# A message-passing layer on one core: an earlier first round of grouped edges, later list and node preparation, three accumulators for four, and four buffers for small sums

## The chip, the cores and the metric

The kernel runs on one core of a Trainium2 chip. The metric is the device time of one execution in microseconds (us). Three runs of the kernel before gave 2089.85, 2090.91 and 2092.94 us, a median of 2090.91. One more execution was recorded by the profiler; all traces below are of such recorded executions.

## What is computed

```python
h = relu(layernorm(x))                      # x: 6250 nodes x 128 features, f32
hw = h @ W_in
W_ij = (softplus(f_ij @ W_f1 + b_f1) - log 2) @ W_f2 + b_f2
W_ij = W_ij * cutoff                        # f_ij: 200000 edges x 20
out = segment_sum(hw[dst] * W_ij, src)      # per edge: gather by dst, sum by src
x + (softplus(out @ W_o1 + b_o1) - log 2) @ W_o2 + b_o2
```

The names follow the kernel's inputs. The list of edges is sorted by `dst`, so the gather of `hw` reads a narrow, moving window of rows. `src` is random, so the sum by `src` goes to rows all over the table of nodes.

## The kernel before

**Units of work.** 128 edges are a chunk, four chunks are a quad (512 edges); there are 391 quads, and one iteration of the main loop starts one quad. Two quads share a load of features, a load of window offsets and four loads of node rows (`load_sc`, L287 to L308), which SP issues two iterations or more ahead.

**A quad's way.** `s1_pe` (L313) multiplies the features with W_f1 in the iteration before; ACT takes exponential and logarithm (L318, L323); `s2_pe_x` and `s2_pe_w` (L494 to L505) gather the node rows by a one-hot matrix and multiply with W_f2; ACT scales by the cutoff (L510); DVE multiplies both (`s2_m`, L520). The message m, 512 edges x 128, is then summed by `src` in one of three ways:

- *Plain quads* (`plainq`): edges with equal `src` within a chunk are summed on PE by an equality matrix (`s3_pe`, L532), copied by ACT (L540), and scattered with addition into an accumulator in HBM: four indirect DMAs issued by POOL (`scatter`, L582).
- *Listed quads*: m goes straight to four such scatters. Edges that repeat a `src` within their column have been given a place in a side list of 128 rows per 16 quads, prepared ahead (`l_eq`, `l_count`, `l_index`, `l_place`) and summed and scattered later (`l_sum`, `l_copy`, with one `os` buffer).
- *Grouped quads*: no scatter of the quad. `src` is cut into 16 groups of 392 nodes. Ranks within a group are prepared for eight quads at once (`rank_group` to `rank_slot`). DVE builds a permutation (`perm_oh`, L662) and splits m into three bf16 parts (`part_rem`, L676), PE permutes the edges so that 32 slots belong to each group (`permute`, L687), and ACT copies (L693). Edges over 32 of a group go to 64 overflow slots (`over_pe`, L702 to L704), are summed in pairs of quads (`over_row`, `over_sum`) and leave as one scatter, through an `os` buffer (`over_copy`, L746). After eight grouped quads, a *round*, four *units* run (`unit_pe`, L781): each adds four groups of all eight quads on PE, and DVE adds the result into `accT` in SBUF (`unit_evac`, L792; L790 in the first round).

So a grouped quad costs matmuls and about half a scatter, and the other kinds cost four scatters and few matmuls.

**Which quad is what.** `sorted_quads` fixes the grouped ones: from 8 on with gaps 2, 2, 2, 3, so 8, 10, 12, 14, 17 and so on to 383, 168 in all; quads 0 to 7 and 384 to 390 are not grouped. `unit_slots` gives the iterations of the units: 28, 32, 37, 41 in the first round, 389, 391, 393, 395 in the last. Of the 223 other quads the middle 192 are listed and 31 are plain (12 at the beginning, 19 at the end).

**What sets the order.** The order on each engine is written out by hand: in iteration i the fixed steps run, and between them hooks at named points (`at(i, point, fn)`; `"L"` for loads, `"D0"` to `"D2"` on DVE, `"PE2"` for the grouped work on PE, `"A0"` to `"A2"` on ACT, `"S"` for scatters). Every engine works strictly in this order. SP issues nearly all loads and stores, POOL the scatters.

**Accumulators.** `NACC = 4` tables of all nodes lie in HBM and take the scatters in turn, so that one scatter does not wait for the landing of the one before (`acc_of`: the first 2 go to table 0, up to 8 to tables 0 and 1, up to 140 to tables 0 to 2, then to all four; the last 64 go to tables 1 to 3, while table 0 is added into `accT` during the loop: `r0_load` to `r0_add`). All are zeroed at the start from a zeroed piece of `accT`: tables 0 and 1 from POOL in the prologue, 2 and 3 by ten SP transfers of 128x640 f32 each (`zero_piece`), the side lists by three each (`zero_list`).

**Preparation of node rows.** `prep_stat` to `prep_x3` normalise 256 nodes, multiply with W_in and write three bf16 parts to a table; the steps of group g start at iteration `prep_start(g)`: 6, 15, 24 and so on for groups 1, 2, 3.

**The end.** After the loop two flags are loaded by every engine (L1272, L1278), which choose fallback code that this input does not need. Then an output stage over 13 groups of 512 nodes loads tables 1 to 3 (`t_load`, L1356), adds them (`t_sum1`, `t_sum2`, L1362, L1368), transposes, adds `accT`, and does the last two layers (L1373 to L1419).

## Time and profile before

| | us |
|---|---|
| runs: lowest, median, highest | 2089.85, 2090.91, 2092.94 |
| the profiled execution's own time | 2069.4 |
| its span, first instruction to last | 2067.6 |
| PE busy | 1854.7 (90%) |
| VectorE (DVE) busy | 1657.1 (80%) |
| POOL busy | 1631.5 (79%) |
| ScalarE (ACT) busy | 1490.1 (72%) |

The span is one execution on the chip, and times in the rows are in us from its start. "busy" is the time in which an engine has an instruction; PE is TensorE's matmuls, PEld its weight loads. In a row of the timeline stand start, length, engine, line, operation, output<-inputs by the program's names, count, and in brackets the idle time before it and what ended it. In a row of waits stand who waited for whom, us in total, how often, and the longest. A group's row gives count, busy us, mean ns of one, and the idle time before.

### The profile page before, as it was taken

How to read it: one execution, taken by the hardware profiler on the slowest of the kernel's cores; microseconds unless marked ns; L12 is line 12 of the kernel's file. 1: busy time of each engine (PE TensorE's matmuls, PEld its weight loads, DVE VectorE, ACT ScalarE, POOL GpSimd, SP SyncE). 2: the span in 40 equal slices, each digit the busy share in tenths (PEclk: the TensorE clock that was granted, in tenths of full speed). 3: DMA queues.
4: the chain of work that ended last, by engine and by line, in shares of the span. 5: the costliest groups of instructions: out<-in, count | busy, mean ns of one | idle time of the engine just before them, and what ended most of it. 6: DMA issues, size and time to landing. Idle time of an engine off the chain costs nothing. (4 is left out here: it accounts for less than half of the span.)

```text
span 2067.6 us, 57535 instructions
## 1 busy us (share of the span) xinstructions
PE 1854.7 (90%) x20381; PEld 1285.7 (62%) x20381; DVE 1657.1 (80%) x4448; ACT 1490.1 (72%) x4083; POOL 1631.5 (79%) x1040
## 2 busy tenths in 40 slices
PE   3489997999999999999999999999999999999956
PEld 2356664666666666666666666666666666677734
DVE  3578896898987888988988978979889787787735
ACT  3368775777776788777778777777778678888714
POOL 3578888888877788887878878888888888888774
PEclk9689998999999999999999999999999999999978
DMA  7887766767766776766667666676676676667648
GB/s 240 227 211 150 125 124 109 128 112 135 130 124 106 126 133 117 136 124 122 121 133 123 122 123 117 118 129 107 129 128 116 112 126 111 110 120 131 129 46 242
DMA packets 381187, 272.56 MB, mean 132 GB/s; under 512 B 97727, under 2 KB 341354, under 8 KB 380898
## 3 DMA queue, kind: packets, MB, share of 16 engines
q0 software_dynamic: 143728, 71.30, 34.9%
q1 hardware_dynamic: 236882, 197.50, 33.8%
q8 instruction: 161, 2.64, 0.5%
q14 instruction: 128, 1.05, 0.2%
q10 hardware_dynamic: 288, 0.07, 0.0%
HBM read 154.45 MB, written 114.24 MB: 130 GB/s over the span
## 5 line engine op out<-in xcount | busy, mean ns | idle before, releaser
L582 POOL DMA_INDIRECT acc<-s,lji x768 | 1237.3, 1611 | 266.9 <-issue 184.6
L687 PE MATMUL pq<-pt,pm 128*128 128x387 bf16 x2688 | 527.9, 339 | 27.0 <-DVE pt L676 10.7
L510 ACT ACTIVATE xc<-xg,cb 128x128 f32<-128x128 f32 x1564 | 446.4, 371 | 121.0 <-PE xg L497 113.8
L505 PE MATMUL W<-w,a 128*128 128x128 f32 x3128 | 464.1, 293 | 0.0
L505 PEld LDWEIGHTS W<-w,a 128*128 128x128 f32 x3128 | 388.7, 196 | 42.0 <-issue 2.6
L781 PE MATMUL un<-so,mst 32*128 32x392 bf16 x8064 | 378.3, 331 | 31.9 <-ACT os L746 19.3
L693 ACT CAST mst<-pq 128x387 bf16<-128x387 f32 x672 | 303.1, 481 | 132.6 <-PE pq L687 130.0
L687 PEld LDWEIGHTS <-pm 128*128 128x128 bf16 x2688 | 259.4, 99 | 211.4 <-issue 16.7
L781 PEld LDWEIGHTS <-mst 32*128 32x128 bf16 x8064 | 228.4, 94 | 175.0 <-issue 70.0
L323 ACT ACTIVATE a<-a,con 128x512 f32<-128x512 f32 x391 | 282.3, 722 | 12.7
L582 POOL DMA_INDIRECT acc<-s,ji x123 | 197.0, 1602 | 82.8 <-issue 25.9
L318 ACT ACTIVATE a<-z 128x512 f32<-128x512 f32 x391 | 237.4, 607 | 33.2 <-PE z L313 17.4
L676 DVE TENSOR_TENSOR pt<-pt 128x512 f32<-128x512 f32 x336 | 231.8, 690 | 5.8
L662 DVE TENSOR_SCALAR pm<-iot,pos 128x576 bf16<-128x576 f16 x672 | 221.4, 390 | 0.0
L520 DVE TENSOR_TENSOR s<-W,xc 128x512 f32<-128x512 f32 x192 | 131.9, 687 | 92.9 <-ACT xc L510 86.0
L792 DVE TENSOR_TENSOR accT<-un,accT 128x392 f32<-128x392 f32 x320 | 158.5, 558 | 58.4 <-PE un L781 58.2
L766 DVE TENSOR_SCALAR so<-iot,mst 128x392 bf16<-128x392 f16 x672 | 191.2, 344 | 5.5 <-PE un L781 5.4
L582 POOL DMA_INDIRECT acc<-os,oji x96 | 155.6, 1621 | 31.1 <-issue 16.2
L497 PE MATMUL xg<-wn,oh 63*128 63x128 bf16 x1564 | 157.2, 222 | 14.5 <-ACT xc L510 8.1
L313 PE MATMUL z<-ft,ws 123*128 123x512 bf16 x391 | 151.6, 388 | 16.1 <-POOL b2rep L927 9.3
L494 PE MATMUL W<-b2rep,onesb 64*128 64x512 bf16 x391 | 153.8, 393 | 0.0
L520 DVE TENSOR_TENSOR pt<-W,xc 128x512 f32<-128x512 f32 x168 | 115.2, 686 | 34.9 <-ACT xc L510 29.4
(209 smaller groups left out, 2431.1 us busy)
## 6 DMA issues: line engine op xcount, KB each, us to landing
rb<-reld SPq DMA_DIRECT2D x391, 64.0 KB
fsd<-f SPq DMA_DIRECT2D x49, 480.0 KB
ft<-fsd SPq DMA_DIRECT2D x195, 120.0 KB
sb<-src SPq DMA_DIRECT2D x169, 128.0 KB
fb<-in_fB_dram SPq DMA_DIRECT2D x49, 320.0 KB
ft<-fsd SPq DMA_DIRECT2D x195, 80.0 KB
wn<-tab SPq DMA_DIRECT2D x782, 15.8 KB
acc<-s,lji POOLq DMA_INDIRECT x768
```

Of the source, the lines that this page charges most:

```text
L318: nc.scalar.activation(a, st[q]["z"], AF.Exp)
L323: nc.scalar.activation(a, a, AF.Ln, bias=half, scale=0.5)
L505: nc.tensor.matmul(W[:, c, :], st[q]["a"][:, c * P:(c + 1) * P], w2, start=False, stop=(c == 3))
L510: nc.scalar.mul(xc[:, c, :], st[q]["xg"][:, c, :], late["c", q // CQ][:, 4 * (q % CQ) + c:4 * (q % CQ) + c + 1])
L520: nc.vector.tensor_tensor(m[:, :, :P], st[q]["W"], st[q]["xc"], op=ALU.mult)
L582: nc.gpsimd.indirect_dma_start(out=accs[k][:rows, :], out_offset=bass.IndirectOffsetOnAxis(ap=ji, axis=0), in_=s, in_offset=None, compute_ ...
L662: nc.vector.tensor_scalar(pm[:, c], iot[:, :SLOTS], rk[r]["pos"][:, 4 * j + c:4 * j + c + 1], None, op0=ALU.is_equal)
L676: nc.vector.tensor_tensor(pt[:, :, k * P:(k + 1) * P], a, high(a), op=ALU.subtract)
L687: nc.tensor.matmul(t[:, :PW], mp[q]["pm"][:, c, s * P:(s + 1) * P], high(mp[q]["pt"][:, c:c + 1, :PW])[:, 0], start=(c == 0), stop=(c == 3))
L693: nc.scalar.copy(mp[q]["ms", s][:, :PW], mp[q].pop(("q", s))[:, :PW])
L766: nc.vector.tensor_scalar(so, iotw[:, :GN], w[:, 3 * P // 2:3 * P // 2 + 1], None, op0=ALU.is_equal)
L781: nc.tensor.matmul(ts[g][:, :GN], mp[q]["ms", s][v, k * P:(k + 1) * P], mp[q]["oh"][v], start=(q == qs[0] and k == 0), stop=(q == qs[-1] a ...
```

## The change

- `HEAD`: quads 2, 3, 5, 6, 8, 9, 11 and 12 are grouped and form the first round. The pattern with gaps 2, 2, 2, 3 begins at 15. There are 176 grouped quads (22 rounds, 88 units) and 215 others: 176 listed, 39 plain (20 at the beginning, 19 at the end). Units of the first round run in iterations 17, 21, 26 and 30; the last grouped quads are 381, 384, 386, 388 and 390, the last units run in 396, 398, 400 and 402. The head quads are permuted within one iteration (`q in HEAD`).
- The ranks of the first round are prepared from iteration 0 on.
- Lists are prepared at their ordinary distance in the first window too, from iteration 12 on (first: 6); node groups start at iteration 22 (first: 6).
- `NACC = 3`. The first 4 scatters go to table 0, up to 24 to tables 0 and 1, then to three; the last 64 go to tables 1 and 2. Table 2 is zeroed one piece per iteration in iterations 3 to 12, lists in 9 to 17.
- `t_sum1` is gone, `t_sum2` is always on POOL, and the output stage loads two tables.
- `os` has four buffers, not two.
- A small load at the start (`half_load`) uses unused columns of `accT` in place of a `pm` buffer.

```diff
+HEAD = (2, 3, 5, 6, 8, 9, 11, 12)
-MP0 = 8
+MP0 = 15
+PREP0 = 23
-NACC = 4
+NACC = 3
...
-    K1_END, K2_END, K3_END = 2, 8, 140
-    Z2, Z3 = [0,0,1,1,2,2,3,3,4,4], [5+2*j for j in range(10)]
+    K1_END, K2_END = 4, 24
+    Z2 = [3+j for j in range(10)]
...
-        w = LR // ZL
-        nc.sync.dma_start(v[:, j * w:(j + 1) * w], zero[:, :w])
+        a, b = j * LR // ZL, (j + 1) * LR // ZL
+        nc.sync.dma_start(v[:, a:b], zero[:, :b - a])
...
-        s = sp_.tile([P, 132], F32, tag="os", name="os", bufs=2)
+        s = sp_.tile([P, 132], F32, tag="os", name="os", bufs=4)
...
-        if k < K3_END:
+        if k < RET:
             return k % 3
-        if k < RET:
-            return k % 4
-        return 1 + k % 3
+        return 1 + k % 2
...
-            t_ = wk.tile([HALF, 2, SEG], I32, tag="pm", name="half")
+            o = NP - 2 * (2 - k) * SEG
+            t_ = accT[:HALF, o:o + 2 * SEG].bitcast(I32).rearrange("p (a e) -> p a e", a=2)
...
-        for j in range(ZR):
-            at(Z3[j] if spread else 0, "L", zero_piece, nc.sync, 3, j)
...
             i = mpq[RKQ * r]
+            i = max(i, 5)
             at(i - 5, "D2", rank_group, r)
...
-                i = splain[n] + 2 if w else 6 + 2 * g
+                i = splain[n] + 2
...
-                    at((0, 3, 6, 9)[k] + j + 1, "L", zero_list, k, j)
+                    at(3 * k + j + 9, "L", zero_list, k, j)
...
-            if q + 4 in units:
+            if q + 4 in units or q in HEAD:
...
-        def t_sum1(g):
-            T = tgroups[g][1]
-            a2 = tl[g][2]
-            nc.gpsimd.tensor_tensor(a2[:, :T], a2[:, :T], tl[g][3][:, :T], op=ALU.add)
...
-            eng = nc.vector if g % 2 else nc.gpsimd
-            eng.tensor_tensor(a1[:, :T], a1[:, :T], tl[g][2][:, :T], op=ALU.add)
+            nc.gpsimd.tensor_tensor(a1[:, :T], a1[:, :T], tl[g][2][:, :T], op=ALU.add)
...
-            for k in (1, 2, 3):
+            for k in (1, 2):
                 t_load(g, k)
...
-    qs, q = [], MP0
+    qs, q, n = [k for k in HEAD if k < nq - MPEND], MP0, 0
     while q < nq - MPEND:
         qs.append(q)
-        q += MPGAPS[(len(qs) - 1) % len(MPGAPS)]
+        q += MPGAPS[n % len(MPGAPS)]
+        n += 1
...
-    busy = unit_its(sorted_quads(4 * PREP_GAP * (g + 8)))
-    return clear(7 + PREP_GAP * (g - 1), busy, 2) - 1
+    busy = unit_its(sorted_quads(4 * PREP_GAP * (g + 10)))
+    return clear(PREP0 + PREP_GAP * (g - 1), busy, 2) - 1
```

More of the change, by code (lines that the diff above doesn't have):

```diff
@@ L744, in over_copy @@
     def over_copy(q):
-        s = sp_.tile([P, 132], F32, tag="os", name="os", bufs=2)
+        s = sp_.tile([P, 132], F32, tag="os", name="os", bufs=4)
         nc.scalar.copy(s[:, :P + 4], mp[q].pop("sum")[:, :P + 4])
@@ L1429, in tile_gnn @@
             if TAIL_AHEAD <= j + TAIL_AHEAD < TG:
-                for k in (1, 2, 3):
+                for k in (1, 2):
                     t_load(j + TAIL_AHEAD, k)
             if j + 1 < TG:
-                t_sum1(j + 1)
                 t_sum2(j + 1)
```

## The prediction

> **What bounds the kernel now.** I read the span first, then a table of busy time by stretch, cut where the pace changes.
>
> ```profile
> span 2067.6 us, 57535 instructions
> ```
>
> ```profile
> 24.40:156.50 132.10, 83.37 (x571) 61.37 (x572) 78.14 (x202) 69.71 (x194) 76.55 (x59) 0.78 0.86 233
> 156.50:344.90 188.40, 176.04 (x1914) 121.04 (x1914) 161.47 (x443) 147.94 (x411) 154.42 (x97) 0.99 0.73 134
> 344.90:377.10 32.20, 17.83 (x197) 11.65 (x194) 14.83 (x48) 13.43 (x40) 25.68 (x18) 0.73 0.51 77
> 377.10:1957.50 1580.40, 1509.93 (x17062) 1044.12 (x17061) 1337.98 (x3600) 1220.77 (x3366) 1299.73 (x806) 0.99 0.69 123
> 1957.50:2013.30 55.80, 32.37 (x469) 22.98 (x467) 23.56 (x68) 8.91 (x31) 42.13 (x28) 0.83 0.42 45
> 2013.30:2067.70 54.40, 33.18 (x173) 23.21 (x173) 27.59 (x45) 25.22 (x39) 24.28 (x20) 0.81 0.87 237
> ```
>
> The columns are the stretch, its length, busy us (and instructions) of PE, PEld, DVE, ACT and POOL, the granted clock, the DMA share and GB/s. From 377.1 on PE is busy 1509.93 of 1580.40 us, 96%. Before that it is not: 63% in the first row, 55% in the third.
>
> The same stretches with only the z matmul of L313, one per iteration (quad), turn lengths into a pace:
>
> ```profile
> 24.40:156.50 132.10, 9.55 (x20) 2.31 (x21) 0.78 0.86 233
> 156.50:344.90 188.40, 15.51 (x40) 4.00 (x40) 0.99 0.73 134
> 344.90:377.10 32.20, 1.14 (x3) 0.30 (x3) 0.73 0.51 77
> 377.10:1957.50 1580.40, 125.02 (x327) 32.80 (x328) 0.99 0.69 123
> ```
>
> An iteration takes 132.1/20 = 6.6 us, then 4.7, then 10.7 (three of them), then 4.83 for the 327 that remain. So PE bounds the long part, and what can be won lies in the first 20 iterations, in the three at 345, and in the two end rows.
>
> The scatters alone (L582, POOL's only large work) show what holds the early part:
>
> ```profile
> 24.40:156.50 132.10, 67.96 (x42) 0.78 0.86 233
> 156.50:344.90 188.40, 154.42 (x97) 0.99 0.73 134
> 377.10:1957.50 1580.40, 1299.73 (x806) 0.99 0.69 123
> ```
>
> 97 scatters in 188.4 us are 1.94 us each and 806 in 1580.4 are 1.96, and POOL has about 0.35 us between two of them in both rows. POOL is nearly full everywhere; what differs is who is late. In the long part the waits show POOL waiting for its data, so PE and DVE lead:
>
> ```profile
> POOL acc L582 <- DVE s L520: 24.7, 19, 3.0
> ```
>
> At 347 it is the other way round, and PE stands still because a small sums buffer has not been scattered yet:
>
> ```profile
> 361.25 0.27 ACT L746 COPY os<-osum 128x132 f32<-128x132 f32 x1 [13.77 <-DMA acc<-os,oji]
> 361.56 6.58 PE L781 MATMUL un<-so,mst 32*128 32x392 bf16 x93 [14.18 <-ACT os L746]
> ...
> ACT os L746 <- DMA acc<-os,oji: 18.2, 2, 13.8
> ```
>
> Both os buffers wait on a POOL that carries the backlog of the first twelve, all scattered, quads. A second such wait, 18.2 - 13.8 = 4.4 us, lies later.
>
> At the end POOL decides again:
>
> ```profile
> 1954.26 1.54 POOL L582 DMA_INDIRECT acc<-s,ji  x1 [2.43 <-ACT ji L563]
> ...
> 1957.59 0.38 PE L313 MATMUL z<-ft,ws 123*128 123x512 bf16 x1
> ...
> 1996.41 1.98 DVE L792 TENSOR_TENSOR accT<-un,accT 128x392 f32<-128x392 f32 x4 [5.27 <-PE un L781]
> ...
> 2006.32 1.54 POOL L582 DMA_INDIRECT acc<-os,oji  x1 [0.30 <-issue]
> 2013.35 25.72 SPq L1356 DMA_DIRECT2D ta_in<-acc  x30
> ```
>
> The last seven quads (384 to 390) are all scattered. From 1954.26 to 2006.32 29 scatters follow each other at 52.1/28 = 1.86 us, while PE and DVE are done at 1998. The first load of the output stage comes 7.0 us after the last scatter started.
>
> **The change part by part.** Prices first, each from the groups of equal shape or, for the twelve overflow matmuls of a quad, from the first and last of them:
>
> ```profile
> L687 PE MATMUL pq<-pt,pm 128*128 128x387 bf16 x2688 | 527.9, 339 | 27.0 <-DVE pt L676 10.7 <-DVE rt L651 6.3 <-ACT mst L693 3.6
> L781 PE MATMUL un<-so,mst 32*128 32x392 bf16 x8064 | 378.3, 331 | 31.9 <-ACT os L746 19.3 <-DVE pr L627 6.8 <-ACT s L540 2.4
> L532 PE MATMUL pp<-m,eq 128*128 128x129 f32 x248 | 36.4, 294 | 18.4 <-DVE m L520 13.0 <-DVE jf L556 2.9 <-DVE jd L552 2.1
> ...
> 118.19 0.25 PE L702 MATMUL po<-pt,pm 128*64 128x131 bf16 x1
> ...
> 118.86 0.22 PE L704 MATMUL po<-pt,pm 128*64 128x128 bf16 x1
> ```
>
> A grouped quad costs PE 527.9/168 = 3.1 us of permuting and 118.19 to 119.08 = 0.9 of overflow, so 4.0; each unit costs 378.3/84 = 4.5 and a round has four; a plain quad's sums cost 36.4/31 = 1.2. One more round (176 grouped quads for 168, 88 units for 84) is 8 x 4.0 + 4 x 4.5 = 50 us of PE, with eight more plain quads, 9 us more. At 96% busy that would be a pure loss if it fell into the long part. It falls elsewhere, so I count it by stretch.
>
> *First 20 iterations, 132.1 us.* By then nine quads are permuted (2, 3, 5, 6, 8, 9, 11, 12, 15) where four were, and one unit (iteration 17) is run: + 5 x 4.0 + 4.5. Seven plain quads fewer: - 7 x 1.2. Net +16, so PE needs 83.4 + 16 = 99 us at the old clock, inside 132. DVE and ACT had 54 and 62 us idle in that row, which take the masks, remainders and copies. What held the stretch was this:
>
> ```profile
> POOL acc L582 <- DMA acc<-s,ji: 22.8, 15, 5.8
> ...
> DVE eql L369 <- DMA sb<-src: 18.8, 5, 9.0
> ```
>
> An iteration with four scatters cannot be shorter than 4 x 1.86 = 7.4 us, and iterations 4 to 11 all had four. Afterwards quads 0, 1, 4, 7, 10 and 13 remain, spread over 14 iterations. The list preparation that stops DVE 18.8 us starts at iteration 12 and not 6. SP is passed by ten zero transfers of the fourth accumulator (320 KB each) and three smaller list zeros fewer, at 233 GB/s about 14 us of a DMA queue that is 86% full; the third accumulator's ten move from iterations 0 to 4 into 3 to 12. What stays is the start-up chain of loads and feature splitting for the first eight quads, and a slow clock (0.78). Bounds: 99 us (no idle left) and 148 (old length plus the 16). I take 122, **-10**, nearer the old row, because the first eight iterations keep their chain.
>
> The new first scatters are narrower: four on accumulator 0 alone, then twenty on two. They are paced at a landing, not at 1.86; with 6 quads in 14 iterations instead of 12 in 12 that is hidden. The first evacuation (iteration 18) overwrites the zeros and so waits for the last list zero, issued at 17; SP issues it ahead of the compute, so I cost it at nothing, and at most a few us.
>
> *Iterations 21 to 63.* Two more units and one permuted quad less: +9 - 4 = **+5**. PE had 93% there, DVE 86%, so this is paid in full.
>
> *The stall at 347.* Four os buffers, and a POOL that is not behind: the three iterations cost 3 x 4.83 = 14.5, not 32.2: **-17.7**. If POOL is behind all the same, nothing.
>
> *The long part.* Two permuted quads more (+8), one unit fewer (-4.5), the second os wait gone (-4.4): -1. Three accumulators for four: the row 156.5 to 344.9 ran on three (scatters 8 to 139 do) at 1.94 us, the long part on four at 1.96, so three cost nothing that can be seen. I take +3. The last 64 scatters rotate over two where they had three. A landing in that part of the trace:
>
> ```profile
> 1965.39 3.61 DMA acc<-s,ji
> ```
>
> Two scatters take 3.7, so a wait of 3.61 + 0.30 - 3.70 = 0.2 per pair, 7 us over 64, is the low end; the early wait of 22.8 us over 42 scatters, 0.54 each, gives 35 as the high one. I take the low end, the nearer row; POOL is not last any more there. Sum **+2**. [...]
>
> *From the last z to the output stage, 55.8 us.* Grouped quads now run to 390. POOL's burst shrinks to four or five quads, each with a PE-paced gap. But PE has, after the last z, three quads to permute (386, 388, 390: 12), five units (390, 396 to 402: 22.5), the last products (6), 40 us in all, and between the last four units nothing fills the wait for evacuation (1.98 in the row of 1996.41) and the next masks (1 us): 3 x 3 = 9, with chain stalls of 4: 53. Then one evacuation (2) and the loading of flags and branches, 7.0 less a landing of 3.6 = 3.4, twice at most: 60 to 62 in all. **+5**, between -5 and +12. What was POOL's end becomes PE's and DVE's.
>
> *Output stage, 54.4 us.*
>
> ```profile
> 2018.53 1.26 POOL L1362 TENSOR_TENSOR ta_in<-ta_in 128x512 f32<-128x512 f32 x1 [10.67 <-DMA ta_in<-acc]
> ...
> 2021.18 1.11 PE L1373 MATMUL tp<-idt,ta_in 128*128 128x128 f32 x4 [23.35 <-POOL ta_in L1368]
> ...
> 2054.91 1.02 PE L1386 MATMUL tz<-oT,wo_sb 128*128 128x512 f32 x2
> ...
> 2055.77 1.06 PE L1409 MATMUL ty<-wo_sb,ta 128*128 128x128 f32 x8
> ...
> 2056.66 0.27 PE L1373 MATMUL tp<-idt,ta_in 128*128 128x128 f32 x1
> ```
>
> Thirteen loads and thirteen sums go. The first transpose comes one sum (1.3) and one load's share (1) earlier. A group takes (2056.66 - 2021.18)/12 = 2.96 us now; PE's own need is about 0.6 + 1.0 + 1.1 = 2.7, so 3 us over twelve. All sums on POOL are 1.3 per group, below that. **-6**, between -2 and -12.
>
> **Sum:** -10 + 5 - 17.7 + 2 + 5 - 6 = **-21.7 us**. The profiled run took 2069.4 (span 2067.6); the median of the runs is 2090.9, 21.5 above, and I carry the difference over unchanged: 2069.2.
>
> **The rivals.**
>
> *Slower: the early matmuls come at half clock on top of an unchanged chain.* Two rows of the same eight matmuls:
>
> ```profile
> 74.61 2.08 PE L505 MATMUL W<-w,a 128*128 128x128 f32 x8
> ...
> 92.59 1.16 PE L505 MATMUL W<-w,a 128*128 128x128 f32 x8
> ```
>
> If the loads still set the pace and the added 16 us run at the slow rate, they cost up to 33 on top of 132: 165 us, 43 more than I forecast, sum +21: 2112. It decides from a first stretch of 122 + 21.7 = 144 us on. For it: DMA 86% full, clock 0.78. Against it: 49 us of PE idle in the row and the scatters that go. [...]
>
> *Two accumulators make POOL the end.* At the high price of 35, less the 13 us by which I see PE end after POOL, the end moves by 22: sum 0, 2091.
>
> *The change does not unload POOL:* the landing-paced start (24 scatters) carries the same backlog to iteration 60 and PE waits there for other buffers. The 17.7 are not won: -4, 2087.
>
> *More:* the first stretch runs near PE's 99 us and the end row gains: -23 - 10 more than forecast at most; about -40, 2051.
>
> **How the numbers follow.** Forecast 0.55 (own range 2058 to 2081), more 0.13, half-clock rival 0.13, two accumulators 0.10, not unloaded 0.09. The range 2050 to 2093 leaves out most of the half-clock rival and a little below. 0.2%, 4 us, is about what a measurement of this kernel can tell from no change. Faster by more: the first two and about half of the two small cases, 0.77; within it 0.10; slower 0.13.
>
> **What would show it.** No wait of ACT os or PE un above 3 us near the 60th z; the 21st z at 145 us or sooner; PE's last unit, not a scatter, ahead of the first output load; 26 loads there; pace of the long part 4.83. Wrong if the first 20 iterations take over 144 us, if the long part's pace rises above 4.9 (23 us), or if the last scatter starts after the last evacuation.

## The result and the profile after

| | kernel before | changed kernel |
|---|---|---|
| 20 runs each: lowest, median, highest (us) | 2078.9, 2087.4, 2096.2 | 2069.9, 2082.4, 2088.6 |
| second group of runs: median | 2069.7 | 2065.0 |
| ratio, first group | | 0.997, interval 0.9957 to 0.9983 |
| ratio, second group | | 0.9981, interval 0.9966 to 0.9996 |
| first profile: span | 2067.6 | 2076.5 |
| profiles of the second group: span | 2062.1 | 2058.3 |

The changed kernel is faster by 4 to 6 us. The forecast was a gain of 21.7.

One thing must be known to read these numbers. The runs fall into groups, each taken together on one chip, and the same kernel has another time in each: the kernel before has medians of 2087, 2072, 2070, 2082, 2084 and 2081 us in the six groups. The two first profiles come from different groups, so their spans (+8.9) say nothing of the change. Ratios are formed inside a group, and the stages are compared in the second group, where both kernels were profiled again (2062.1 and 2058.3: -3.8).

The z matmuls are counted from 0, as the quads are. The stretches of the first profile after, cut near the first, at the 20th, 60th, 75th and 390th z matmul, at the first load of the output stage and at the end (columns as before):

```profile
span 2076.5 us, 58773 instructions
```

```profile
24.40:138.90 114.50, 89.19 (x706) 61.68 (x707) 79.27 (x200) 76.81 (x209) 54.34 (x45) 0.96 0.76 208
138.90:342.10 203.20, 193.43 (x2204) 136.63 (x2202) 176.75 (x487) 160.08 (x455) 161.55 (x99) 1.00 0.69 126
342.10:417.20 75.10, 67.98 (x762) 47.81 (x760) 65.04 (x187) 55.53 (x156) 61.18 (x39) 1.00 0.68 117
417.20:1981.20 1564.00, 1473.00 (x16504) 1013.36 (x16503) 1298.77 (x3498) 1176.36 (x3264) 1250.65 (x773) 0.98 0.68 120
1981.20:2033.10 51.90, 43.50 (x626) 28.17 (x623) 30.22 (x92) 14.75 (x44) 36.03 (x23) 0.95 0.36 33
2033.10:2076.50 43.40, 30.16 (x173) 22.55 (x173) 24.28 (x39) 24.71 (x39) 15.69 (x13) 0.81 0.81 222
```

The first 20 iterations are shorter by 18 us and their clock is 0.96 in place of 0.78. There is no 14 us stall any more. The long part is what changed against expectation: 315 iterations in 1564.0 us, 4.97 each, where the forecast had 4.83 and named 4.9 as a sign of being wrong. The same stretches of the second group, the kernel before first, the 20th to 60th and the 75th to 390th z:

```profile
155.50:347.20 191.70, 179.26 (x1934) 123.55 (x1933) 163.63 (x449) 149.14 (x414) 157.69 (x98) 0.98 0.70 133
...
433.80:1952.30 1518.50, 1448.98 (x16413) 1001.37 (x16413) 1286.90 (x3472) 1174.80 (x3241) 1252.82 (x776) 0.99 0.68 123
```

```profile
137.40:340.30 202.90, 194.42 (x2204) 136.87 (x2202) 177.36 (x487) 160.67 (x455) 161.06 (x98) 0.99 0.67 126
...
417.80:1962.70 1544.90, 1467.03 (x16504) 1011.36 (x16503) 1296.07 (x3497) 1179.38 (x3263) 1243.13 (x772) 0.98 0.66 121
```

All stages of this pair (lengths from the starts of the z matmuls):

| stage | before | changed | difference | forecast |
|---|---|---|---|---|
| first to 20th z | 131.1 | 113.7 | -17.4 | -10 |
| 20th to 60th | 191.7 | 202.9 | +11.2 | +5 |
| 60th to 75th (the stall) | 86.6 | 77.5 | -9.1 | -17.7 |
| 75th to 390th (the long part) | 1518.5 | 1544.9 | **+26.4** | **+2** |
| last z to first output load | 55.4 | 52.0 | -3.4 | +5 |
| output stage | 54.4 | 43.6 | -10.8 | -6 |
| start of the first z | 24.4 | 23.7 | -0.7 | 0 |

At the end the order is as forecast, in the first profile after. The last scatter now precedes the last evacuation, and the first load follows 3.0 us after that:

```profile
2026.02 1.54 POOL L582 DMA_INDIRECT acc<-os,oji  x1 [0.63 <-issue]
...
2028.17 1.98 DVE L792 TENSOR_TENSOR accT<-un,accT 128x392 f32<-128x392 f32 x4 [3.00 <-PE un L781]
2033.14 0.93 SPq L1356 DMA_DIRECT2D ta_in<-acc  x2
```

### The profile page after: what moved, and what is told of

It reads as the page before. It is cut to its first block, busy times and chain, and to the rows that moved or that the text cites. A ratio compares the mean times of both kernels' runs of the same rounds, so it can differ in the third digit from the quotient of the medians.

```text
span 2076.5 us, 58773 instructions
## 1 busy us (share of the span) xinstructions
PE 1899.2 (91%) x20971; PEld 1311.5 (63%) x20971; DVE 1687.2 (81%) x4541; ACT 1512.3 (73%) x4168; POOL 1587.7 (76%) x1005
## 5 line engine op out<-in xcount | busy, mean ns | idle before, releaser
L582 POOL DMA_INDIRECT acc<-s,lji x704 | 1137.8, 1616 | 264.1 <-issue 162.7
L687 PE MATMUL pq<-pt,pm 128*128 128x387 bf16 x2816 | 563.6, 343 | 58.8 <-DVE pt L676 13.8
L507 PE MATMUL W<-w,a 128*128 128x128 f32 x3128 | 456.9, 289 | 0.0
L693 ACT CAST mst<-pq 128x387 bf16<-128x387 f32 x704 | 318.9, 482 | 176.2 <-PE pq L687 139.3
L687 PEld LDWEIGHTS <-pm 128*128 128x128 bf16 x2816 | 273.9, 100 | 264.4 <-issue 61.8
L507 PEld LDWEIGHTS W<-w,a 128*128 128x128 f32 x3128 | 382.1, 192 | 41.2 <-issue 1.0
L781 PE MATMUL un<-so,mst 32*128 32x392 bf16 x8448 | 387.1, 326 | 6.5 <-ACT os L746 1.3
L582 POOL DMA_INDIRECT acc<-s,ji x156 | 255.4, 1637 | 132.2 <-DMA acc<-s,ji 51.6
L781 PEld LDWEIGHTS <-mst 32*128 32x128 bf16 x8448 | 238.7, 93 | 148.4 <-issue 48.8
L676 DVE TENSOR_TENSOR pt<-pt 128x512 f32<-128x512 f32 x352 | 242.8, 690 | 6.0
L662 DVE TENSOR_SCALAR pm<-iot,pos 128x576 bf16<-128x576 f16 x704 | 234.2, 393 | 0.0
L522 DVE TENSOR_TENSOR s<-W,xc 128x512 f32<-128x512 f32 x176 | 120.9, 687 | 80.0 <-ACT xc L512 52.4
L499 PE MATMUL xg<-wn,oh 63*128 63x128 bf16 x1564 | 155.2, 220 | 12.3 <-ACT xc L512 7.8
```

The lines of the kernel that those rows point to most:

```text
L507: nc.tensor.matmul(W[:, c, :], st[q]["a"][:, c * P:(c + 1) * P], w2, start=False, stop=(c == 3))
L522: nc.vector.tensor_tensor(m[:, :, :P], st[q]["W"], st[q]["xc"], op=ALU.mult)
L582: nc.gpsimd.indirect_dma_start(out=accs[k][:rows, :], out_offset=bass.IndirectOffsetOnAxis(ap=ji, axis=0), in_=s, in_offset=None, compute_ ...
L662: nc.vector.tensor_scalar(pm[:, c], iot[:, :SLOTS], rk[r]["pos"][:, 4 * j + c:4 * j + c + 1], None, op0=ALU.is_equal)
L676: nc.vector.tensor_tensor(pt[:, :, k * P:(k + 1) * P], a, high(a), op=ALU.subtract)
L687: nc.tensor.matmul(t[:, :PW], mp[q]["pm"][:, c, s * P:(s + 1) * P], high(mp[q]["pt"][:, c:c + 1, :PW])[:, 0], start=(c == 0), stop=(c == 3))
```

## The experiments

Each ratio is to the kernel before in the same group of runs. "The 66th z" is the stretch from the start of the 66th z matmul to that of the 67th. It holds the grouped work of iteration 65, since s1_pe runs one iteration ahead.

### First group: which part of the change does it

**The kernel before again.** No edit. 

> The kernel before, unchanged, timed against itself and profiled once more. Its ratio should be 1.000. Theory A (three accumulators slow the long part) needs the second profile of the kernel before to run from the 135th to the 390th z matmul in about 1222 us, as the first did, against 1270 us of the changed kernel. Theory B (the first profile of the kernel before was an unusually quick execution, 18 us below the median of its runs, and the long part of the changed kernel is an ordinary one) expects about 1222 + 18 = 1240 us or more there in a second profile whose time is near the median of 2087 us.

Ratio 0.9993 (0.9978 to 1.0008), span 2065.3. Its 135th to 390th z took 1221.7 us, as Theory A needs, and not the 1240 of Theory B; its 75th to 375th took 1449.0 us, the first profile's 1451.7. The long part of the kernel before is steady.

**Three accumulators alone**, in the kernel before:

```diff
-NACC = 4
+NACC = 3
-    K1_END, K2_END, K3_END = 2, 8, 140
+    K1_END, K2_END = 2, 8
...
-        return 1 + k % 3
+        return 1 + k % 2
```

> The kernel before with three accumulators in place of four (the ten zero transfers and three list zeros of the fourth, its loads and its sums in the output stage go with it), two os buffers and the old pattern kept. Theory A: the output stage gives 10 us back, the long part loses 30 to 48 us: slower than before by 20 to 38 us, ratio 1.010 to 1.018. Theory B: the output stage gives 10 us, the long part costs about 3 as forecast: ratio 0.995 to 0.998.

Ratio 1.007 (1.0047 to 1.0092): slower, 15 us, but not by Theory A's way. Up to the 315th z this kernel is as far as the kernel before (1598.2 and 1597.6 us), so three in rotation cost nothing. The loss is late: waits for an os buffer between the 315th and the 360th quad (ACT's copies waited 13.7 us for one from the 75th to the 375th z, 4.4 in the kernel before), and above all the last 64 scatters on two tables, which make POOL the end:

```profile
2022.02 1.98 DVE L790 TENSOR_TENSOR accT<-un,accT 128x392 f32<-128x392 f32 x4 [5.15 <-PE un L779]
...
2040.67 5.00 SPq L1352 DMA_DIRECT2D ta_in<-acc  x8
```

The first load comes 16.7 us after the last evacuation (2024.0); the last z to that load takes 70.6 us where the kernel before has 55.8. That is my rival "two accumulators make POOL the end". It holds for the old pattern, whose last seven quads are all scattered, and not for the new one.

**Four os buffers alone**, in the kernel before:

```diff
-        s = sp_.tile([P, 132], F32, tag="os", name="os", bufs=2)
+        s = sp_.tile([P, 132], F32, tag="os", name="os", bufs=4)
```

The same edit stands in `l_copy` and in `over_copy`. 

> The kernel before with four os buffers for two and nothing else. If the stall near the 60th quad is worth its length, the time falls by 17.7 to 22 us, ratio 0.990, and the profile has no wait of ACT os above 3 us there. If POOL's backlog only moves the wait to the next buffer (s of the plain and listed quads, or DVE m), the ratio is 0.998 to 1.000 and the z matmul that follows the old stall by 60 quads is as late as before.

Ratio 0.996 (0.9947 to 0.9973), between the two expectations. The wait near the 60th quad did not go. It moved to the next instruction on ACT that needs a buffer which the same scatter holds, the index `oji` with its two buffers:

```profile
367.03 0.29 ACT L755 ACTIVATE oji<-ojd,con 128x1 int32<-128x1 f32 x1 [14.11 <-DMA acc<-os,oji]
```

14.11 us in place of 13.77, and the 60th to 75th z take 82.1 us as in the repeated profile of the kernel before (83.1). What the buffers gain is the second wait of my forecast: the 300th to 330th z take 138.2 us in place of 145.1.

**Four accumulators in the changed kernel** (the fourth zeroed in iterations 8 to 17):

```diff
-NACC = 3
+NACC = 4
+        for j in range(ZR):
+            at(8 + j, "L", zero_piece, nc.sync, 3, j)
...
-        return 1 + k % 2
+        return 1 + k % 3
```

> The changed kernel with four accumulators again (the fourth zeroed by ten transfers in iterations 8 to 17, list zeros in 6 to 17, used from the 60th scatter on; three loads and two sums per group in the output stage); head round, later preparation and four os buffers kept. Theory A: the long part gains 30 to 48 us against the changed kernel, the output stage loses 10, the added 3.3 MB of zeros cost 0 to 10: 2045 to 2070 us, ratio to the kernel before 0.980 to 0.992. Theory B: no gain in the long part beyond 3 us, so 2085 to 2100 us, ratio 0.999 to 1.006.

Ratio 1.0038 (1.0023 to 1.0054). **Theory A falls.** The 75th to 375th z take 1475.9 us with four tables, and 1481.1 and 1465.9 with three in the two profiles of the changed kernel; the three come from three groups of runs, but a gain of 30 to 48 us is not there. What the fourth costs is elsewhere: the 20th z comes at 145.6 (137.4 with three), the output stage takes 53.7 (43.6). Theory B named the wrong reason too: the loss of the long part is no accident of one profile.

### Second group: where the long part loses

**The changed kernel again.** No edit. 

> The changed kernel, unchanged, timed and profiled once more. In the first experiments the kernel before ran at 2072 us on the chip, where it had 2087 us beside the changed kernel, and its second profile agreed with its first within 3 us at every quad. If the execution on another chip moves both kernels alike, the ratio to the kernel before is 0.997 again. If the kernel before alone moved, and its profile is the ordinary one for the chip on which the first experiments ran, the changed kernel is at 2076 to 2084 us beside 2072 us there: ratio 1.002 to 1.006.

Ratio 0.9981, shown above: both kernels move with the group.

**The kernel before, a third time.** No edit. 

> One more look at the kernel before, on the chip of this group of runs. If its time is near 2070 us its z matmuls are within 3 us of the first two profiles all along; if it is near 2087 us the profile shows in which stretch 15 us come in: in one stall (the wait near the 60th quad, or the one between quads 315 and 330), or evenly with the clock.

2063.9 us, span 2062.1; its 75th to 375th z took 1445.6. Its 315th z comes at 1592.9 us, 5 to 7 us ahead of the first two profiles and not within 3.

**Without the head round**, from the version with four accumulators:

```diff
-HEAD = (2, 3, 5, 6, 8, 9, 11, 12)
+HEAD = ()
-LEARLY = 8
+LEARLY = 20
```

> The changed kernel without the head round (grouped quads 15, 17, 19, 21, 24 and on, 168 of them, quads 0 to 14 all scattered; 28 plain quads at the beginning), with four accumulators and four os buffers; the pattern, lists and node groups from iteration 40 on stand where the changed kernel has them. Theory C (the long part is slower because the pattern now begins at 15, so that it meets the loads and hooks of even iterations and the later node groups otherwise): from the 75th to the 375th z matmul 1470 to 1480 us, as in the changed kernel (1481) and its version with four accumulators (1476). Theory D (the head round itself leaves something behind, a POOL or ACT that is late): 1448 to 1455 us, as in the kernel before. Its first 75 quads should be slower than those of both, since 15 quads are scattered at the start: 450 to 480 us at the 75th z.

Ratio 1.018 (1.0158 to 1.0203), the 75th z at 451.6. The long part is that of the changed kernel: 1470.6 us from the 75th to the 375th. **Theory C holds, Theory D falls**: the pattern's place costs, with all that moves with it (lists and node groups), and not the head round. The stall near the 60th z is gone here too: without the head round the longest iteration from the 40th to the 75th z is the 66th. POOL's lag is paid earlier, 155.1 us for the first 20 z where the kernel before has 131.1. Here the 234th to 378th z of three kernels, 144 iterations or eight rounds, equal in grouped quads and units: the kernel before, the changed one, and this one.

```profile
1213.90:1893.60 679.70, 654.48 (x7446) 450.89 (x7444) 567.13 (x1483) 528.54 (x1449) 567.96 (x354) 0.99 0.67 120
```

```profile
1207.10:1898.80 691.70, 662.54 (x7465) 454.88 (x7462) 570.67 (x1494) 530.56 (x1461) 567.78 (x351) 0.98 0.66 118
```

```profile
1245.30:1937.10 691.80, 663.58 (x7475) 457.23 (x7472) 569.18 (x1495) 531.54 (x1461) 568.77 (x354) 0.98 0.66 119
```

19 matmuls of some 7450 more, and 12 us more time: 8 of busy PE, 4 of idle, and a granted clock of 0.98 in place of 0.99. Folded by the round's 18 iterations, two of them stand out against the first profile of the kernel before: the 15th after the pattern's begin takes 9.4 us on average and not 6.5, and the first 4.5 and not 3.3 (a list sum at the 340th z, 9.3 us); most others are a little shorter. At the 15th the single values alternate: 14.8 us at the 66th z, 6.1 at the 84th, 12.7 at the 102nd, 6.1 at the 120th, 16.2 at the 138th, and so on to the 318th.

**Four os and four oji buffers** in the kernel before, the edit of the os buffers above and this one:

```diff
-        ji = sp_.tile([P, 1], I32, tag="oji", name="oji", bufs=2)
+        ji = sp_.tile([P, 1], I32, tag="oji", name="oji", bufs=4)
```

> The kernel before with four os and four oji buffers. With four os buffers alone ACT waited 14.1 us for an oji buffer at the place where it had waited 13.8 us for an os buffer. If that wait is what holds PE there, the 60th to 75th quads now take 70 to 74 us and not 82 to 86, and the time falls by 8 to 12 us more than the 9.6 of four os buffers: ratio 0.990 to 0.992. If the backlog of POOL is what sets the pace, the wait moves on to the next buffer (s of the scattered quads) and the ratio stays at 0.995 to 0.997.

Ratio 0.9931 (0.9909 to 0.9953). The 60th to 75th z take 70.0 us, the stall is gone, and with it 13 us at the 75th z. So the stall is worth about what I gave it, but it takes both buffers.

### Third group: the collision

What alternates is the counting of the lists. Worked out from the hooks, and seen in the traces, `l_count` falls into the iteration of `rank_count` in iterations 29, 65, 101 and so on to 317, nine times, in the changed kernel and never in the kernel before. The eight from 65 on are looked at here.

**Lists one iteration later**, in the changed kernel:

```diff
-                i = splain[n] + 2
+                i = splain[n] + 3
```

> The changed kernel with the lists prepared one iteration later (splain[n] + 3 for + 2) and nothing else. Theory E (the pattern that begins at 15 moves the counting of the lists, 16 matmuls of L380 behind two comparisons of 1.2 us on DVE, into the same iteration as the rank counting of every second round, L612: iterations 65, 101, 137 and so on to 317, eight of them, where an iteration took 9 to 17 us and not 6.1): one iteration later they miss each other as in the kernel before, the iterations 66, 102, 138, 210, 282 take 6 to 9 us, the 234th to 378th z matmul 672 to 680 us (changed kernel 692, kernel before 678 to 681), and the time falls by 15 to 40 us against the changed kernel: ratio to the kernel before 0.979 to 0.991. Theory F (the work in those iterations has to be done anyway and PE only spends it elsewhere): 234th to 378th z 688 to 693 us, ratio 0.997 to 0.999.

Ratio 0.994 (0.9917 to 0.9962), 6 to 9 us better than the changed kernel, less than Theory E asked. The 66th, 102nd, 174th, 210th, 246th and 318th z fall to 8.2 us and less; the 138th and the 282nd stay at 17.8 and 17.9, with a granted clock of 0.62 in both, and the 234th to 378th z took 699.5, as if nothing were won there. Neither theory had that.

**Lists two iterations earlier**, in the kernel before, so that they meet:

```diff
-                i = splain[n] + 2 if w else 6 + 2 * g
+                i = splain[n] if w else 6 + 2 * g
```

> The kernel before with its lists prepared two iterations earlier (splain[n] for + 2), so that counting of lists and of ranks meet in one iteration of every second round (76, 112, 148 and so on to 328, eight). Theory E: the same loss as in the changed kernel, 234th to 378th z 690 to 698 us in place of 678 to 681, slower by 15 to 40 us, ratio 1.007 to 1.019. Theory F: ratio 0.998 to 1.002.

Ratio 1.0056 (1.0035 to 1.0078), 12 us slower, and 686.7 us from the 234th to the 378th z. That is a loss, as Theory E says, but less than its 15 to 40 us. The 77th, 113th, 149th, 185th, 221st, 257th, 293rd and 329th z, 6.1 to 7.9 us in the kernel before, take 9.8 to 12.3. This is the cleanest sight of the waiting. The PE of the kernel before at the 149th z, then of this one:

```profile
797.38 0.38 PE L313 MATMUL z<-ft,ws 123*128 123x512 bf16 x1
...
798.15 0.44 PE L741 MATMUL osum<-mo,oeq 128*128 128x132 f32 x2
798.52 3.01 PE L687 MATMUL pq<-pt,pm 128*128 128x387 bf16 x16
...
803.61 0.38 PE L313 MATMUL z<-ft,ws 123*128 123x512 bf16 x1
```

```profile
811.64 0.38 PE L313 MATMUL z<-ft,ws 123*128 123x512 bf16 x1
...
812.40 0.54 PE L378 MATMUL lcnt<-wgtb,eql 128*128 128x1 bf16 x16
812.80 0.47 PE L741 MATMUL osum<-mo,oeq 128*128 128x132 f32 x2
814.18 0.87 PE L687 MATMUL pq<-pt,pm 128*128 128x387 bf16 x4 [0.90 <-DVE pt L676]
815.62 0.86 PE L687 MATMUL pq<-pt,pm 128*128 128x387 bf16 x4 [0.57 <-ACT mst L693]
817.06 0.86 PE L687 MATMUL pq<-pt,pm 128*128 128x387 bf16 x4 [0.57 <-ACT mst L693]
818.49 0.86 PE L687 MATMUL pq<-pt,pm 128*128 128x387 bf16 x4 [0.57 <-issue]
```

The whole stretch of this 149th z, in the columns of the tables above:

```profile
811.60:821.40 9.80, 7.18 (x66) 4.56 (x66) 8.41 (x26) 3.38 (x9) 7.97 (x7) 1.00 0.72 133
```

Sixteen permuting matmuls that ran through in 3.01 us come in fours, and each four after the first stands 0.57 us; for two of the three the profile names ACT's copy of an earlier four as what ended it. The granted clock is 1.00, so this is waiting alone. The reason is in the code: all these results are tiles of one tag, which take turns in four buffers of the pool `ps` in PSUM, where this program's matmuls write.

```python
t = ps.tile([P, 512], F32, tag="B", name="lcnt", bufs=4)
```

`rkp`, `osum` and `pq` have the same tag. The first two are held until the next iteration, when DVE and ACT come to them; with `lcnt` that makes three, and one buffer is left for permuting.

**Lists one later and four oji buffers**, in the changed kernel: both edits above. 

> The changed kernel with the lists one iteration later and four oji buffers. In the changed kernel ACT waited 5 to 11 us for oji buffers, in the kernel before, with four os buffers, 20.0; there four oji buffers took another 10 us. If Theory E holds this is the fastest of all, 2 to 8 us below the kernel with the lists later: ratio 0.976 to 0.989. If Theory F holds 0.995 to 0.998.

Ratio 0.995 (0.9933 to 0.9967), Theory F's figure and not Theory E's: the buffers add nothing that can be told. In the changed kernel the waits for oji were 5 to 12 us in all.

**Two os buffers** in the changed kernel (4 to 2 in both places). 

> The changed kernel with two os buffers again. If the head round alone takes the backlog from POOL (plain and listed quads are scattered 6 to 16 us after their data, where it was 15 to 24 before the 60th quad), the two buffers suffice: no wait of ACT os over 4 us near the 60th quad, ratio to the kernel before as with four, 0.997 to 0.999. If the four buffers are needed, 4 to 12 us slower than the changed kernel: ratio 1.000 to 1.004.

Ratio 1.0013 (0.9993 to 1.0034), 7 to 9 us slower than with four. But the 60th to 75th z take 77.5 us, as with four: the rest of the change removes the stall without the os buffers. That the head round does it is not shown, since the kernel without it, with four os buffers, has no stall there either. The waits come later, the longest at the 315th z, which takes 15.7 us:

```profile
ACT os L746 <- DMA acc<-os,oji: 12.3, 4, 8.3
```

### Fourth and fifth group: order in time, or order in the iteration

**Lists and their sums one iteration later**, in the changed kernel:

```diff
-            i = clear(wend[w] + 12, units)
+            i = clear(wend[w] + 13, units)
```

> The changed kernel with the lists prepared one iteration later and their sums one iteration later too (wend + 13 for + 12), so that neither falls into an iteration of the rank counting. Theory G (the list sums in iterations 137 and 281 are a second collision): iterations 138 and 282 take 6 to 9 us and not 17.8, the 234th to 378th z 680 to 688 us, and the time falls by another 5 to 15 us: ratio 0.987 to 0.992. Theory H (what is left is spread over the pattern and not in collisions): 234th to 378th z 690 to 700, ratio 0.993 to 0.996.

Ratio 0.9934 (0.9909 to 0.9958), no more than without, and 693.2 us from the 234th to the 378th z: Theory H's figures. The 138th and 282nd z fall to 11.3 and 11.4; others rise.

**The same with four oji buffers.** 

> The same with four oji buffers. With four os buffers in the kernel before, four oji were worth 10 us; in the changed kernel with the lists later they were worth nothing that the timing could tell (0.995 beside 0.994). Both theories expect the ratio of the run without them, within 0.002.

Ratio 0.994 (0.9919 to 0.9962).

**Sums two iterations later**, in the kernel before (`wend[w] + 14`), so that three meet the rank counting. 

> The kernel before with the sums of its lists two iterations later (wend + 14), so that three of them (iterations 58, 202 and 346) fall into the rank counting. Theory G: iterations 203 and 347 take 12 to 18 us where they took 6.1 to 6.3, and the time rises by 8 to 25 us, ratio 1.004 to 1.012. Theory H: ratio 0.998 to 1.002.

Ratio 0.999 (0.9973 to 1.0007). The 203rd and 347th z do take 10.0 and 12.6 us in place of 6.3 and 6.1, but three such iterations are too few to show in the time. Theory G is right on the place and wrong on the size.

**Lists behind the permuting**, in the changed kernel. Nothing changes its iteration; `l_count` and `l_sum` are only issued behind the permuting and overflow matmuls:

```diff
-                at(i, "PE2", l_count, (LB + SW * w) // 4 + g)
+                at(i, "A2", l_count, (LB + SW * w) // 4 + g)
...
-            at(k, "PE2", l_sum, w)
+            at(k, "A2", l_sum, w)
```

> The changed kernel with the products of the list counting and of the list sums issued behind the permuting and overflow matmuls of the same iteration, not ahead of them; nothing else is moved. Theory P (PSUM buffers of tag B: three of four are held by small results while PE permutes): iterations 66, 102, 138, 174, 210, 246, 282 and 318 fall from 9.5 to 17 us to 6 to 9, the 234th to 378th z to 678 to 687 us (changed kernel 692), and the time by 8 to 25 us: ratio to the kernel before 0.985 to 0.994. Theory Q (DVE's load in those iterations, rank preparation and list comparison together, is what holds them): they stay at 9 us and more, 234th to 378th z 690 to 696, ratio 0.996 to 0.999.

Ratio 0.9865 (0.9848 to 0.9882): 28 us faster than the kernel before, some 22 to 24 beyond the changed kernel. It takes 689.0 us from the 234th to the 378th z, between the two theories. PE at the 66th z, in the changed kernel (second profile) and here:

```profile
365.08 0.38 PE L315 MATMUL z<-ft,ws 123*128 123x512 bf16 x1
366.76 0.38 PE L612 MATMUL rkp<-G,tri 128*128 128x512 bf16 x1 [1.30 <-DVE G L599]
...
367.30 0.54 PE L380 MATMUL lcnt<-wgtb,eql 128*128 128x1 bf16 x16
367.71 0.47 PE L741 MATMUL osum<-mo,oeq 128*128 128x132 f32 x2
369.18 0.87 PE L687 MATMUL pq<-pt,pm 128*128 128x387 bf16 x4 [1.00 <-DVE pt L676]
370.62 1.45 PE L687 MATMUL pq<-pt,pm 128*128 128x387 bf16 x4 [0.57 <-ACT mst L693]
372.65 1.45 PE L687 MATMUL pq<-pt,pm 128*128 128x387 bf16 x4 [0.57 <-ACT mst L693]
374.68 1.45 PE L687 MATMUL pq<-pt,pm 128*128 128x387 bf16 x4 [0.57 <-ACT mst L693]
...
378.03 2.08 PE L507 MATMUL W<-w,a 128*128 128x128 f32 x8
379.90 0.63 PE L315 MATMUL z<-ft,ws 123*128 123x512 bf16 x1
```

```profile
363.81 0.38 PE L315 MATMUL z<-ft,ws 123*128 123x512 bf16 x1
...
367.96 4.47 PE L687 MATMUL pq<-pt,pm 128*128 128x387 bf16 x16 [1.43 <-DVE pt L676]
...
373.19 0.55 PE L380 MATMUL lcnt<-wgtb,eql 128*128 128x1 bf16 x16
...
375.00 0.38 PE L315 MATMUL z<-ft,ws 123*128 123x512 bf16 x1
```

The two stretches as a whole:

```profile
365.10:379.90 14.80, 10.78 (x67) 6.41 (x64) 11.12 (x34) 5.96 (x16) 12.66 (x8) 0.68 0.61 97
363.80:375.00 11.20, 8.42 (x66) 5.09 (x65) 10.71 (x30) 5.35 (x14) 9.49 (x6) 0.85 0.57 103
```

The fours are gone, with DVE's work in that iteration nearly the same (11.12 and 10.71 us), and the granted clock rises from 0.68 to 0.85. The eight long z of Theory P's list took 109.1 us together in the changed kernel and take 84.2 here. They fall to 7.9 to 13.0 and not all to 6 to 9: PE still waits for DVE there (1.43 us for the remainders of L676 at this place), Theory Q's share. In the ratio Theory P holds.

**Rank counting behind as well, four oji buffers**, in the changed kernel. 

> The changed kernel with the list counts, list sums and rank counts all issued behind the permuting, and four oji buffers. Theory P: the permuting of every round's rank iteration has four or three buffers, some 1 to 5 us beyond the run before: ratio 0.983 to 0.992. Theory Q: 0.994 to 0.998, and the rank counting may come late for its reader on DVE, which costs 1 us in each of 21 rounds: up to 1.008.

Ratio 0.9918 (0.9903 to 0.9933): within Theory P's range, but 11 us worse than the run before it where it should have been better. In its trace PE waits 41.3 us for DVE's remainders (L676) ahead of the permuting, 21.1 in the run before. The four oji buffers brought nothing in the two runs above, so the rank counts seem better left ahead.

**The same in the kernel before**, with four os and four oji buffers. 

> The kernel before with four os and four oji buffers and the same three products behind the permuting. In the kernel before they meet the permuting less, so Theory P expects 0 to 6 us less than with the buffers alone (0.993): ratio 0.990 to 0.993. Theory Q: 0.992 to 1.002.

Ratio 0.985 (0.9832 to 0.9867), the fastest of all, 2049.4 us beside 2081.3, and without any part of the change but the os buffers. It is more than either theory asked beside the 0.9931 of the buffers alone. The two profiles, of different groups, do not show where: the 75th to 390th z take 1515.2 and 1515.6 us. So the move, with the rank counts in it, is worth some 17 us in a kernel whose list and rank counts never meet, and the 22 to 24 us of the changed kernel cannot be put down to the collision alone.

## Why the prediction was wrong

**The step that failed is "The long part … Sum +2".** It counted matmuls and accumulators, and took the waiting between engines and the granted clock as unchanged. They do not stay: the pattern's begin moved from 8 to 15 and the lists with it, and so the hooks of two periods, 18 iterations for a round and 36 for five list counts, met anew. Measured +26.4 us: PE's idle time rose by 8.4 us (69.5 to 77.9) and its busy time by 18.1 (1448.98 to 1467.03), with 91 matmuls of 16413 more. The busy time holds the larger part, and the clock, 0.98 in place of 0.99 over the part, can account for it by the estimate behind the next rows. The collisions at the 102nd, 138th, 210th, 246th and 282nd z of the changed kernel (second profile), and last the 131st z of the kernel before, which stands at the same place of its round as the 138th:

```profile
543.30:556.00 12.70, 9.72 (x67) 5.51 (x65) 8.94 (x27) 3.43 (x9) 10.54 (x7) 0.73 0.55 86
722.20:738.40 16.20, 11.02 (x75) 7.02 (x72) 10.39 (x32) 4.90 (x12) 12.39 (x8) 0.68 0.59 96
1083.70:1098.80 15.10, 10.39 (x67) 5.76 (x66) 11.97 (x34) 4.87 (x12) 7.86 (x6) 0.66 0.47 84
1261.30:1275.40 14.10, 11.00 (x67) 6.29 (x66) 9.19 (x28) 4.20 (x12) 11.66 (x9) 0.64 0.48 55
1434.90:1451.90 17.00, 10.82 (x74) 6.96 (x72) 11.38 (x33) 4.84 (x12) 14.25 (x10) 0.70 0.55 87
...
709.10:716.70 7.60, 6.52 (x51) 4.16 (x50) 7.39 (x28) 3.43 (x9) 6.38 (x5) 1.00 0.86 150
```

Length times the missing share of the clock is 24 us over these five rows. That is an estimate of the most that the clock can have cost there, since a part of it fell into PE's idle time.

Shown is that the place of the pattern costs this without the head round (1470.6 us from the 75th to the 375th z, beside 1465.9 with it and 1445.6 in the kernel before), that the iterations in which the counts meet are the ones that grow (109.1 us for eight of them in the second profile, 52.2 for the eight at the same place in the third profile of the kernel before, which hold no list count), and that making the same two products meet in the kernel before costs 12 us. There the clock stayed at 1.00 in seven of the eight, so that run repeats the waiting and not the clock. Not shown is that the meeting explains all 26.4 us, or how they divide. Moving the lists brought 6 to 9 us back, and with the sums moved too, so that nothing meets the ranks, 7 to 10 in all; in that trace the clock of the long part is back at 0.99, but PE still idles 84.7 us of it. Issuing the list products behind the permuting brought some 22, but the same move with the rank counts gains some 17 where nothing meets. So a part of the loss lies in the pattern outside these collisions, as Theory H had it, and stays open. Everything needed to see the meeting stood in the code before the run: a table of the hooks per iteration, before and after, has nine coincidences in the one column and none in the other.

The other steps, in the forecast's order:

- *First 20 iterations*, -10: -17.4. Right in kind, the bound of 99 was nearer than that of 148. PE's added work showed as 4 us of busy time and not 16, while the clock rose from 0.78 to 0.97. The half-clock rival went the other way: its slow row (74.5 to 76.8 us of the first profile before) has a granted clock of 0.50 and its other row 1.00, but the stretch as a whole sped up.
- *Iterations 21 to 63*, +5: +11.2. I took seven plain quads away in the first 20 iterations and forgot that the plain beginning now lasts longer. By the matmuls of their line, eight each, the changed kernel runs eight plain quads in the first 20 iterations, four fewer than the kernel before, and twelve more from the 20th to the 60th z. No permuted quad is missing there either, with 288 permuting matmuls in both. Of plain quads the kernel before has none here; in the second profile of the changed kernel they are the row of L534, 12.79 us of PE:

```profile
137.40:340.30 202.90, 12.79 (x96) 12.58 (x96) 0.99 0.67 126
```

- *The stall*, -17.7: -9.1 over the 60th to 75th z. The stall itself went, and the run with four os and four oji buffers puts its price at 16.6 us (86.6 less 70.0). But the 66th z of the changed kernel is one of the collisions, 14.8 us. I also credited two causes at once. The runs part them: four os buffers alone only hand the wait to `oji`, the rest of the change is enough here without them, and the os buffers pay later (7 to 9 us).
- *Three accumulators*, "nothing that can be seen": right, four are not faster in the long part. The first profile after does have more POOL waits for a landing, 53.5 and 35.8 us where the kernel before had 24.9 and 24.2. They made Theory A likely, but the fourth table, which takes many of them away, made nothing faster:

```profile
POOL acc L582 <- DMA acc<-s,ji: 53.5, 44, 4.4
POOL acc L582 <- DMA acc<-s,lji: 35.8, 78, 1.7
```

- *The last 64 on two*, 7: the last 15 iterations take 78.9 and 82.8 us in the two profiles of the changed kernel and 76.3 with four tables, so 3 to 7. The low end was the right one to choose, but it is not in my sum: the +2 is -1 and +3. With it the forecast would have been -14.7.
- *The end row*, +5: -3.4. PE's 43.3 us of work are as summed (40), but between the units it waits far less than the 13 us that I put in, and the flags cost 3.0 us once.
- *Output stage*, -6: -10.8, within its bounds.
- *Carrying the profile to the median*: as a difference it held in the second group, where the spans differ by 3.8 us and the medians by 4.6. The 21.5 us themselves did not carry over: the first profile of the changed kernel lies 4.1 us below its median. Both kernels move with the group of runs, by up to 18 us.

The sign was right and for the stated reasons: the early part, the stall and the end together gave 41.4 us (17.4 + 9.1 + 3.4 + 10.8 + 0.7), the middle row took 11.2 and the long part 26.4 of it back. That a gain was left is in part luck: the first 20 iterations, the end row and the output stage gave 21 us more than I had for them.

## What to carry to other kernels

When the order is written by hand and parts of it repeat with different periods, moving one part by a few iterations changes which products meet; list the hooks per iteration before and after, and look for iterations in which one rotating pool must serve more results than it has buffers. A small result that waits for its reader in the next iteration holds a whole buffer, so issue it behind the large ones that need the pool (here the ratio went from 0.9981 to 0.9865). And before giving an engine more buffers at the place where it waits, look at what else the same transfer holds: here the wait of 13.77 us for `os` became one of 14.11 us for `oji`.

## What the hardware showed beside this

In the 66th z above, after short waits of PE, some matmuls took longer than the same ones elsewhere. The second four of the permuting takes 1.45 us where the first took 0.87, and the products of L507 after it 2.08 where they take 1.16 at the 66th z of the run with the lists behind the permuting. The gaps ahead of the rank counting, the first four and each later four are 1.30, 1.00 and 0.57 us, and the granted clock of the stretch is 0.68. At the 149th z of the kernel whose lists meet, with gaps of 0.90 and 0.57 us and none ahead of the rank counting, every four stays at 0.86 or 0.87, and the clock at 1.00. Whether the gaps lowered the clock, and which of them, was not tried.

That one kernel differs between groups of runs by up to 18 us in its median, and the changed kernel's two profiles by 18.2 us of span, was not expected either. Of these 18.2, 19.1 lie in the 75th to 390th z, 13 of them as idle PE (91.0 and 77.9 us); what makes the groups differ was not tried. The chip alone does not seem to: the groups with 2070 and 2082 us bear the same chip number.
